# First phase of a transformer-and-experts kernel: block 0 of the token tiles is queued freely, the router's weight parts lie side by side, transposes get one more slot, TensorE gets filler matmuls at its start

## The chip, the cores and the metric

The kernel runs on one core of a Trainium2 chip. Its time is the device time of one execution in microseconds (us). A core has five engines that run side by side, each through its own instructions in their order: TensorE (PE, matmuls; the rows PEld are its weight loads), VectorE (DVE), ScalarE (ACT), GpSimd (POOL) and SyncE (SP, which here only issues DMA transfers). They wait for one another by semaphores.

## The reference

The input is 4096 tokens of width 256. Three residual steps follow each other: a mixture of experts, attention, and the same mixture again.

```python
x = x + 0.5 * ffn(layernorm(x), router_w, rg, ru, rd, sg, su, sd)
x = x + attn(layernorm(x), w_qkv, ln_w, w_proj)
x = x + 0.5 * ffn(layernorm(x), router_w, rg, ru, rd, sg, su, sd)

def ffn(x, ...):                                  # 8 experts, 2 per token, capacity 640
    xn = x * rsqrt(mean(x * x) + eps)
    probs = softmax(xn @ router_w.T)
    top 2 of probs, their weights normalised to a sum of 1
    per expert e, its first 640 tokens in order:
        eout = (silu(xg @ rg[e]) * (xg @ ru[e])) @ rd[e], times the token's weight
    routed = those rows added to their tokens
    shared = (silu(x @ sg) * (x @ su)) @ sd       # sg, su: 256 x 2048, sd: 2048 x 256
    return shared + routed
```

Attention works in groups of 64 tokens with 16 heads of width 16, a causal mask, and normalised queries and keys.

## The kernel before

All matmuls run in float16 on numbers that are split in two: a high half `hi`, rounded to float16, and a low half `lo`, the rounded rest. `split` makes both from a float32 tile (ScalarE the high half, L105; VectorE the low half, L106). A product is the sum of three of the four products of halves, `TERMS`: hi by hi, hi by lo, lo by hi.

The kernel has four phases. Phase a takes the tokens in 32 tiles of 128, which form 8 blocks of 4 tiles. Each tile is loaded (L669), normalised, transposed into the block's buffer `xb` (hi of two column halves, then lo of both), and routed. In the same phase the shared feed-forward runs for the blocks 0 to 3. Phase b is the 8 experts, phase c attention of the 32 tiles together with shared blocks 4 to 7 and the second router, phase d the experts again and the last shared block.

The shared feed-forward (`shared`) goes through 16 steps `c` for a block. A step has gate and up matmuls (`pgu`, L337, twelve of 512 columns), then `sl` by ScalarE (silu, L348) and VectorE (L350), `hh` and `hl` (the split of `sl`, L352 and L353), and the twelve down matmuls of the step before it (`po`, L361).

A tile of phase a goes through `tile1` and `front_steps`. `stats` computes mean and variance on VectorE (`st` L145, `mv` L146, `ve` L148) and the reciprocal root on POOL (`rstd` L150); `normed` makes `z` (L162). The four tiles of block 0 (`PEB = 1`) are then transposed by TensorE: `turn` makes two transposes into `ptx` (L186), a ScalarE copy of the high half (L187) and a VectorE subtraction for the low half (L188). Every later tile is written by `two` as halves into `X` (L169, L170) and transposed by a DMA that SP issues (`flip`, L179); two yields later `logits` multiplies it with the router's weights `rwt` (`pl`, L637, six matmuls of 8 columns per tile) and ScalarE copies the result into `L` (L224). After four tiles `route` picks the two experts of each token (L240, L241 and on), computes weights on POOL and the places in the experts' buffers, and POOL scatters the rows (L318).

The order of the work has two sources. The program yields between steps, and `Tiles.steps` and `drive` let several tiles advance by one step each between the steps of the shared feed-forward. Then the build's planner (`schedule_with_timeline_sim=True`) sets the order of each engine's instructions by its own estimates. It is bound by the data, and by `issue_after`: what is built inside `behind(True, 0, 1)` may not stand ahead of the two instructions in `self.latest`. `turn` sets `latest` to its ScalarE copy and its VectorE subtraction; later the feed-forward sets it (L348, L350). In `Tiles.steps` every step of every tile is put behind `latest` as soon as there is one, that is from the second tile's statistics on.

PSUM has three buffers for gate and up matmuls, two for `po` in this phase, and three shared by `ptx`, `pl`, the router's small matmuls and the transposed router weights `prt`. `rwt` is a tile of [128, 2, 2, 8]: before the change the first index of the two is the part (hi, lo), the second the half of the 256 columns.

The shared weights are loaded and split in eight portions by `load_shared`, the first at once from ScalarE's DMA queue, the others from SP's queue, which also carries the token tiles.

Of the kernel before, what the change touches and what calls it, by code (L numbers as in the profile page):

```python
# [8 lines left out]
F32 = mybir.dt.float32  # L9
# [6 lines left out]
ALU = mybir.AluOpType  # L16
# [4 lines left out]
P = 128  # L21
# [8 lines left out]
E = 8  # L30
# [4 lines left out]
TERMS = ((0, 0), (0, 1), (1, 0))  # L35


class Net:
# [70 lines left out]
    def load_router(self, router_w):  # L109
        nc = self.nc  # L110
        r = self.raw.tile([E, H], F32, name="rtr", bufs=1)
        nc.sync.dma_start(out=r, in_=router_w)
        self.rwt = self.cst.tile([P, 2, 2, E], F16, name="rwt")
        p = self.m1([P, 2, E], F32, "prt")
        for k in range(2):
            nc.tensor.transpose(p[:, k, :], r[:, k * P:(k + 1) * P], self.ident[:E, :E])
        self.split(self.rwt[:, 0], self.rwt[:, 1], p)

    def load_shared(self, sg, su, sd):

# [54 lines left out]
    def flip(self, xp, xt=None):  # L175
# [3 lines left out]
        self.nc.sync.dma_start_transpose(out=xt, in_=xp[:, 0:2 * H])  # L179
        return xt  # L180

    def turn(self, z, xt):

        p = self.m1([P, 2, P], F32, "ptx")
        for k in range(2):
            self.nc.tensor.transpose(p[:, k, :], z[:, k * P:(k + 1) * P], self.ident)  # L186
        i = self.nc.scalar.copy(xt[:, 0:2], p)  # L187
        j = self.nc.vector.tensor_tensor(out=xt[:, 2:4], in0=p, in1=xt[:, 0:2], op=ALU.subtract)  # L188
        self.latest = [i.ins, j.ins]

    @contextmanager
    def behind(self, on=True, *engines):
# [24 lines left out]
    def logits(self, fb, t, xt):  # L217

        nc = self.nc
        p = self.m1([P, E], F32, "pl")  # L220
        self.project(p, lambda a, k: xt[:, 2 * a + k, :], self.rwt, TERMS)
        if t == 0:
            fb["L"] = self.sm.tile([P, 4, E], F32, name="L")
        nc.scalar.copy(fb["L"][:, t, :], p)  # L224

    def route(self, R, b, fb):

        nc = self.nc
        sm = self.sm
        mv, rstd = fb["mv"], fb["rstd"]  # L230
        rs = sm.tile([P, 4], F32, name="rs")
        nc.gpsimd.tensor_tensor(out=rs, in0=rstd, in1=rstd, op=ALU.mult)
        nc.gpsimd.tensor_tensor(out=rs, in0=rs, in1=mv[:, :, 1], op=ALU.mult)
        nc.gpsimd.tensor_scalar_add(rs, rs, RMS_EPS * UP ** 2)
        nc.gpsimd.tensor_tensor(out=rs, in0=rs, in1=self.mhalf[:, :4], op=ALU.pow)
        L = fb["L"]
        mx = sm.tile([P, 4, E], F32, name="mx")
        ix = sm.tile([P, 4, E], U32, name="ix")
        for t in range(4):
            nc.vector.max(out=mx[:, t, :], in_=L[:, t, :])  # L240
            nc.vector.max_index(out=ix[:, t, :], in_max=mx[:, t, :], in_values=L[:, t, :])  # L241
        dl = sm.tile([P, 4], F32, name="dl")
        nc.vector.tensor_tensor(out=dl, in0=mx[:, :, 1], in1=mx[:, :, 0], op=ALU.subtract)
        nc.gpsimd.tensor_tensor(out=dl, in0=dl, in1=rs, op=ALU.mult)
        nc.gpsimd.tensor_scalar_mul(dl, dl, 1.0 / WS)
        nc.gpsimd.tensor_tensor(out=dl, in0=self.e1, in1=dl, op=ALU.pow)
        w1 = sm.tile([P, 4], F32, name="w1")
        nc.gpsimd.tensor_scalar_add(w1, dl, 1.0)
        nc.gpsimd.tensor_tensor(out=w1, in0=w1, in1=self.mone, op=ALU.pow)
        nc.gpsimd.tensor_scalar_mul(w1, w1, 0.5 / WS)  # L250
        nc.gpsimd.tensor_tensor(out=dl, in0=dl, in1=w1, op=ALU.mult)
        nc.gpsimd.tensor_tensor(out=w1, in0=w1, in1=dl, op=ALU.subtract)
        ef = sm.tile([P, 4, 2], F32, name="ef")
        nc.vector.tensor_copy(ef, ix[:, :, 0:2])
        yield
        oh = sm.tile([P, 4, 2, E], F32, name="oh")
        nc.vector.tensor_tensor(
            out=oh, in0=ef.unsqueeze(3).to_broadcast([P, 4, 2, E]),
            in1=self.iota8.unsqueeze(1).unsqueeze(1).to_broadcast([P, 4, 2, E]), op=ALU.is_equal)
        M = sm.tile([P, 4, E], BF16, name="M")  # L260
        nc.vector.tensor_tensor(out=M, in0=oh[:, :, 0, :], in1=oh[:, :, 1, :], op=ALU.add)
        yield
        pp = self.m1([P, 4, E], F32, "pp")
        nc.tensor.matmul(pp, lhsT=self.tri, rhs=M, start=True, stop=False)
        for t in range(1, 4):
            nc.tensor.matmul(pp[:, t:4], lhsT=self.ones, rhs=M[:, 0:4 - t], start=False, stop=False)
        nc.tensor.matmul(
            pp, lhsT=self.ones, rhs=R["run"].unsqueeze(1).to_broadcast([P, 4, E]), start=False, stop=True)
        n4 = sm.tile([P, E], F32, name="n4")
        nc.vector.tensor_reduce(out=n4, in_=M.rearrange("p t e -> p e t"), axis=AX.X, op=ALU.add)  # L270
        nc.vector.tensor_tensor(out=R["run"], in0=R["run"], in1=n4, op=ALU.add)
        pk = sm.tile([P, 4, 2, E], F32, name="pk")
        nc.vector.tensor_tensor(
            out=pk, in0=oh, in1=pp.unsqueeze(2).to_broadcast([P, 4, 2, E]), op=ALU.mult)
        pos = sm.tile([P, 4, 2], F32, name="pos")
        nc.vector.tensor_reduce(out=pos, in_=pk, axis=AX.X, op=ALU.add)
        yield
        df = sm.tile([P, 4, 2], F32, name="df")
        nc.vector.scalar_tensor_tensor(
            out=df, in0=ef, scalar=float(CAP), in1=pos, op0=ALU.mult, op1=ALU.add)  # L280
        nc.vector.tensor_scalar(
            out=pos, in0=pos, scalar1=float(CAP), scalar2=8192.0, op0=ALU.is_ge, op1=ALU.mult)
        nc.vector.tensor_tensor(out=df, in0=df, in1=pos, op=ALU.add)
        di = sm.tile([P, 4, 2], I32, name="di")
        nc.vector.tensor_copy(di, df)
        yield
        if b == NB - 1:
            self.limits(R)
            yield
        for t in range(4):  # L290
            with self.tc.issue_after(self.anchor.ins) if self.anchor else nullcontext():
                self.scatter(R, b, fb, t, di, w1, dl, ef)
            yield
# [346 lines left out]
    def front_steps(self, y, t, new_fb, keep=None):  # L640
        fb = new_fb(t)
        self.stats(y, fb["mv"][:, t, :], fb["rstd"][:, t:t + 1])
        yield
        X = self.xs.tile([P, XW], F32, name="X")
        xp = X[:, 0:H].bitcast(F16)
        fb["X"][t] = X
        z = self.normed(y, fb["mv"][:, t, :], fb["rstd"][:, t:t + 1], keep is not None)
        xt = fb["xb"][:, :, t * P:(t + 1) * P]
        if fb["pe"]:
            self.turn(z, xt)  # L650
            fb["n"] += 1
            for _ in range((3 - t) * GAP_A + 1):
                yield
        with self.behind(fb["pe"], 0, 1):
            self.two(xp, z, keep is not None)
        if keep is not None:
            self.nc.sync.dma_start(out=keep, in_=y)
        yield
        if not fb["pe"]:
            self.flip(xp, xt)  # L660
            yield
            yield
        self.logits(fb, t, xt)
        fb["n"] += not fb["pe"]
        yield
# [7 lines left out]
class Tiles:  # L673
# [12 lines left out]
    def steps(self):  # L686

        if self.slot == self.nxt * self.gap and self.nxt < self.count:
            self.live.append(self.make(self.nxt))
            self.nxt += 1  # L690
        for g in list(self.live):
            with self.held.behind(self.held.latest is not None, 0, 1) if self.held else nullcontext():
                r = next(g, "end")
            if r == "end":
                self.live.remove(g)
            elif r == "stall":
                return
            yield
        self.slot += 1
# [10 lines left out]
def run_slots(tiles, until):  # L710
    while not until():
        for _ in tiles.steps():
            pass
# [22 lines left out]
def macaron(ctx, tc, x, w_qkv, ln_w, w_proj, router_w, rg, ru, rd, sg, su, sd, out):  # L736
    nc = tc.nc
    x = x.rearrange("b s h -> (b s) h")
    out = out.rearrange("b s h -> (b s) h")
    n = Net(ctx, tc)  # L740
# [47 lines left out]
    with n.phase("a", BT, 2, 16):  # L788
        n.ident = n.at.tile([P, P], F32, name="ident")
        make_identity(nc, n.ident)  # L790
        weights = n.load_shared(sg, su, sd)
        next(weights)
        n.load_router(router_w)
        tiles = Tiles(tile1, 32, GAP_A, n)
        run_slots(tiles, ready(1, 0))
        next(weights)
        for b in range(NA):
            run_slots(tiles, ready(1, b))
            main = all_shared((1, b), b, x, R1["acc"])
            drive(fed(main, weights) if b == 0 else main, tiles, RATE_A)  # L800
        run_slots(tiles, tiles.done)
# [26 lines left out]
PEB = 1  # L828
# [29 lines left out]
```

## Time and profile before

| what | value |
|---|---|
| median of 3 runs | 1824.61 us (1823.98 to 1827.08) |
| profiled execution, its own time | 1828.36 us |
| profiled execution, span from first to last instruction | 1826.6 us |
| busy: TensorE, VectorE, ScalarE, POOL | 97%, 66%, 52%, 41% |
| first gate matmul of the shared feed-forward | 17.57 us |
| first gate matmul of an expert in phase b | 284.2 us |
| DMA engines, mean busy share up to 17.57 us | 0.81 |

The profile is of one execution. Its times count from the start of the span. A row of the timeline has the start (us), the time until the last of its instructions ends (us), engine, source line, operation, what is written and read, how many instructions of the kind are in the row, and in brackets how long the engine idled before and what ended that. `L337` is line 337 of the kernel before. Matmuls overlap in the records, so that the time from one start to the next is the better measure of one. A row of the view by windows has the stretch (us), its length, the busy time and count of TensorE, its weight loads, VectorE, ScalarE and POOL, the share of TensorE's full clock that was granted, the DMA engines' busy share, and GB/s.

### The profile page before, as it was taken

Reading aid. Unit: us, or ns where it says so; the run is one execution under the profiler, and the core shown is the slowest. Engines: PE = TensorE matmul, PEld = TensorE weight load, DVE = VectorE, ACT = ScalarE, POOL = GpSimd, SP = SyncE. Lnnn points to the kernel's source line nnn. Section 1 sums busy time; section 2 is a strip of 40 time slices with the busy share of each in tenths; the row PEclk is TensorE's granted clock in tenths of the full one; section 3 lists DMA queues with packets and bytes.
Section 4 is the critical chain, followed back from the end, with each engine's and each line's share of the span. In section 5 each row is a group of like instructions: output and inputs, shape, how many; then the busy total and the mean of one; then the engine's idle time right before and its main releaser. Section 6 shows DMA issues by size and latency. Waiting matters only on the chain.

```text
span 1826.6 us, 37514 instructions
## 1 busy us (share of the span) xinstructions
PE 1778.0 (97%) x13724; PEld 1197.1 (66%) x13724; DVE 1198.9 (66%) x2891; ACT 951.6 (52%) x2055; POOL 754.5 (41%) x1072
## 2 busy tenths in 40 slices
PE   6999999999999899999999999999999999999998
PEld 3555657777777556666666666666655677777765
DVE  6665545666666567787777877887756566666643
ACT  4433334555555466666666666666333455555542
POOL 4666630122111334566767676776430011113210
PEclk9999999999999999999999999999999999999999
DMA  6244132455443356767576776756213144455420
GB/s 196 80 114 114 32 88 63 108 125 120 115 108 87 83 82 99 134 111 148 118 144 118 133 146 117 144 100 130 51 28 73 32 111 108 111 122 122 102 44 12
DMA packets 439193, 185.95 MB, mean 102 GB/s; under 512 B 302305, under 2 KB 436125, under 8 KB 439008
## 3 DMA queue, kind: packets, MB, share of 16 engines
q1 hardware_dynamic: 420528, 161.60, 40.8%
q0 software_dynamic: 17664, 21.17, 6.5%
q8 instruction: 107, 1.75, 0.4%
q10 hardware_dynamic: 816, 0.79, 0.1%
q14 instruction: 78, 0.64, 0.1%
HBM read 78.95 MB, written 42.21 MB: 66 GB/s over the span
## 4 chain that ended last, share of the span: by engine, by line
PE 47%; issue 21%; POOL 12%; DVE 10%; DMA 5%; ACT 3%; SPq 1%; another core or an unknown queue 1%; POOLq 0%; DVEq 0%; ACTq 0%
PE pgu L337 29%; PE po L361 15%; POOL xg L318 3%; DVE sl L350 2%; DMA acc<-eo,eidscatter 2%; DVE sl L345 1%; DVE hl L353 1%; POOL X L316 1%; POOL rstd L150 1%; POOL acc L460 1%; PE pqk L637 1%; POOL S L584 1%; POOL xa L170 1%; ACT sl L344 1%
## 5 line engine op out<-in xcount | busy, mean ns | idle before, releaser
L337 PE MATMUL pgu<-xb,sgu 128*128 128x512 f16 x3072 | 742.2, 380 | 15.5 <-DVE sl L345 8.6
L352 ACT CAST hh<-sl 128x512 f16<-128x512 f32 (+2 forms) x512 | 273.1, 534 | 481.5 <-DVE sl L350 465.5
L337 PE MATMUL pgu<-xe,wc 128*128 128x384 f16 (+1 forms) x3072 | 497.0, 299 | 0.0
L337 PEld LDWEIGHTS <-sgu 128*128 128x128 f16 x3072 | 293.4, 98 | 291.7 <-issue 24.2
L350 DVE SCALAR_TENSOR_TENSOR sl<-pgu,sl 128x512 f32<-128x512 f32 (+2 forms) x512 | 300.7, 588 | 244.8 <-PE pgu L337 213.3
L353 DVE TENSOR_TENSOR hl<-sl,hh 128x512 f16<-128x512 f32 (+2 forms) x512 | 310.8, 607 | 152.6 <-ACT hh L352 147.2
L361 PEld LDWEIGHTS <-hh 128*128 128x128 f16 x3328 | 320.8, 98 | 107.9 <-ACT hh L352 7.3
L337 PEld LDWEIGHTS <-wc 128*128 128x128 f16 x3072 | 300.6, 98 | 92.0
L361 PE MATMUL po<-sdw,hh 128*128 128x256 f16 x2048 | 350.0, 273 | 3.4 <-ACT hh L352 2.2
L361 PE MATMUL po<-sdw,hl 128*128 128x256 f16 x1024 | 247.6, 273 | 6.6 <-DVE hl L353 5.9
L361 PE MATMUL po<-wd,hh 128*128 128x256 f16 x1280 | 223.6, 273 | 0.0
L460 POOL DMA_INDIRECT out_dram<-eo,eidscatter x40 | 65.2, 1629 | 341.5 <-DVE eo L459 331.8
L348 ACT ACTIVATE sl<-pgu 128x384 f32<-128x384 f32 (+1 forms) x336 | 158.9, 473 | 73.0 <-PE pgu L337 43.8
L361 PEld LDWEIGHTS <-hl 128*128 128x128 f16 x1664 | 162.8, 98 | 48.5 <-DVE hl L353 14.7
L460 POOL DMA_INDIRECT acc<-eo,eidscatter x40 | 66.2, 1655 | 293.4 <-DVE eo L459 283.7
L318 POOL DMA_INDIRECT xg<-X,di x128 | 131.3, 1026 | 54.8 <-issue 27.8
L361 PE MATMUL po<-wd,hl 128*128 128x256 f16 x640 | 152.5, 273 | 0.6 <-DVE hl L353 0.6
L345 DVE SCALAR_TENSOR_TENSOR sl<-sl,pgu 128x512 f32<-128x512 f32 x176 | 120.0, 682 | 48.1 <-ACT sl L344 46.9
L344 ACT ACTIVATE sl<-pgu 128x512 f32<-128x512 f32 x176 | 104.2, 593 | 44.9 <-PE pgu L337 35.4
L105 ACT ACTIVATE wc<-re 128x512 f16<-128x512 f32 x128 | 80.5, 629 | 68.9 <-PE pgu L337 59.4
L106 DVE SCALAR_TENSOR_TENSOR wc<-re,wc 128x512 f16<-128x512 f32 x128 | 88.3, 690 | 22.0 <-ACT wc L105 21.8
L584 POOL TENSOR_TENSOR S<-S,amx 128x1024 f32<-128x1024 f32 x32 | 62.1, 1939 | 79.0 <-DVE amx L583 72.0
(150 smaller groups left out, 1713.6 us busy)
## 6 DMA issues: line engine op xcount, KB each, us to landing
re<-in_L_ffn_rg_dram SPq DMA_DIRECT2D x128, 128.0 KB
re<-in_L_ffn_ru_dram SPq DMA_DIRECT2D x128, 128.0 KB
re<-in_L_ffn_rd_dram SPq DMA_DIRECT2D x128, 128.0 KB
y<-acc SPq DMA_DIRECT2D x64, 128.0 KB
y<-in_L_attn_x_dram SPq DMA_DIRECT2D x32, 128.0 KB
acc<-xr SPq DMA_DIRECT2D x16, 256.0 KB
out_dram<-xr SPq DMA_DIRECT2D x16, 256.0 KB
x<-y SPq DMA_DIRECT2D x28, 128.0 KB
```

What stands on the lines that cost most here:

```text
L105: nc.scalar.mul(hi, src, WS)
L106: nc.vector.scalar_tensor_tensor(out=lo, in0=src, scalar=WS, in1=hi, op0=ALU.mult, op1=ALU.subtract)
L318: i = nc.gpsimd.indirect_dma_start(out=R["xg"][:, :], out_offset=bass.IndirectOffsetOnAxis(ap=di[:, t, k:k + 1], axis=0), in_=X, in_offset ...
L337: nc.tensor.matmul(p, lhsT=wc[:, w, i, k, :], rhs=x[:, 2 * a + k, :], start=(j == 0), stop=(j == 5))
L344: nc.scalar.activation(s, p, AF.Tanh, scale=0.5 / XP)
L345: nc.vector.scalar_tensor_tensor(out=s, in0=s, scalar=1.0, in1=p, op0=ALU.add, op1=ALU.mult)
L348: self.latest[0] = nc.scalar.activation(s, p, AF.Silu, scale=1.0 / XP).ins
L350: self.latest[1] = nc.vector.scalar_tensor_tensor(out=s, in0=ps[1], scalar=1.0 / XP / (2.0 * XP if tanh else 1.0), in1=s, op0=ALU.mult, op ...
L352: nc.scalar.copy(h[0], s)
L353: nc.vector.tensor_tensor(out=h[1], in0=s, in1=h[0], op=ALU.subtract)
L361: nc.tensor.matmul(o, lhsT=h[a][:, t * P:(t + 1) * P], rhs=wd[:, w], start=(c == 0 and j == 0 and t % 2 == 0), stop=(c == nch - 1 and j == 2),
L460: i = nc.gpsimd.indirect_dma_start(out=R["acc"][:, :], out_offset=bass.IndirectOffsetOnAxis(ap=ids[:, t:t + 1], axis=0), in_=eo, in_offset ...
```

## The change

- `Tiles.steps` keeps each tile's number and puts its steps behind `latest` for tiles of block 1 and later; the tiles of block 0 are not held.
- `rwt` is laid out with the column half first, so that its high and low parts are neighbours. `logits` multiplies the high half of a tile with both parts at once (16 columns), and the low half with the high part (8 columns): four matmuls per tile. The two partial sums stay apart in `L`; `route` adds them with one VectorE instruction per block.
- A tile of phase a that is transposed by DMA waits three yields, not two, before its logits. Tiles of phase c keep two.
- `keep_going(n)` issues n matmuls of the constant tile `ones` (128 columns, bfloat16) into a buffer that nothing reads: 20 before the router's weights are transposed, 16 after, and 5 after each `turn`, 56 in all.

```diff
@@ load_router
-        self.split(self.rwt[:, 0], self.rwt[:, 1], p)
+        self.split(self.rwt[:, :, 0], self.rwt[:, :, 1], p)
@@ Net
+    def keep_going(self, n):
+        p = self.m1([P, P], F32, "idle")
+        for _ in range(n):
+            self.nc.tensor.matmul(p, lhsT=self.ones, rhs=self.ones, start=True, stop=True)
@@ turn
         self.latest = [i.ins, j.ins]
+        self.keep_going(5)
@@ logits
-        p = self.m1([P, E], F32, "pl")
-        self.project(p, lambda a, k: xt[:, 2 * a + k, :], self.rwt, TERMS)
+        p = self.m1([P, 2, E], F32, "pl")
+        for k in range(2):
+            nc.tensor.matmul(
+                p, lhsT=xt[:, k, :], rhs=self.rwt[:, k], start=(k == 0), stop=False, skip_group_check=True)
+            nc.tensor.matmul(
+                p[:, 0], lhsT=xt[:, 2 + k, :], rhs=self.rwt[:, k, 0], start=False, stop=(k == 1),
+                skip_group_check=True)
         if t == 0:
-            fb["L"] = self.sm.tile([P, 4, E], F32, name="L")
-        nc.scalar.copy(fb["L"][:, t, :], p)
+            fb["L"] = self.sm.tile([P, 4, 2, E], F32, name="L")
+        nc.scalar.copy(fb["L"][:, t], p)
@@ route
-        L = fb["L"]
+        L = sm.tile([P, 4, E], F32, name="Ls")
+        nc.vector.tensor_tensor(out=L, in0=fb["L"][:, :, 0], in1=fb["L"][:, :, 1], op=ALU.add)
@@ front_steps
             self.flip(xp, xt)
-            yield
-            yield
+            for _ in range(2 if keep is not None else 3):
+                yield
@@ Tiles.steps
-            self.live.append(self.make(self.nxt))
+            self.live.append((self.nxt, self.make(self.nxt)))
             self.nxt += 1
-        for g in list(self.live):
-            with self.held.behind(self.held.latest is not None, 0, 1) if self.held else nullcontext():
-                r = next(g, "end")
+        for one in list(self.live):
+            with self.held.behind(one[0] >= 4 * PEB, 0, 1) if self.held else nullcontext():
+                r = next(one[1], "end")
             if r == "end":
-                self.live.remove(g)
+                self.live.remove(one)
@@ macaron, phase a
         next(weights)
+        n.keep_going(20)
         n.load_router(router_w)
+        n.keep_going(16)
         tiles = Tiles(tile1, 32, GAP_A, n)
```

## The prediction

> **What bounds the kernel now.** I read the page first: TensorE is busy 97% of the span, and in the row of slices only the first slice (45.7 us each) is clearly below 9.
>
> ```profile
> span 1826.6 us, 37514 instructions
> PE 1778.0 (97%) x13724; PEld 1197.1 (66%) x13724; DVE 1198.9 (66%) x2891; ACT 951.6 (52%) x2055; POOL 754.5 (41%) x1072
> PE   6999999999999899999999999999999999999998
> ```
>
> So time is won only where TensorE waits, runs at a low clock, or has work taken off it. The diff touches the first phase (to 284.2 us, where the first expert's gate matmul starts) and, through `logits` and `route`, the attention phase. The waits of TensorE in two windows, 0 to 17.6 us and 17.6 to 284.2 us (us in total, times, longest), come next:
>
> ```profile
> PE ptx L186 <- DVE z L162: 11.4, 4, 3.0
> ...
> PE pgu L337 <- DVE sl L350: 4.2, 5, 1.5
> PE pl L637 <- DMA xb<-X: 3.3, 4, 2.1
> ```
>
> The 11.4 us are the four tiles of block 0, taken one behind the other. The timeline shows one turn of that chain, and where the real work begins:
>
> ```profile
> 4.01 0.43 DVE L145 BATCH_NORM_STATS2 st<-y 128x6 f32<-128x256 f32 x1 [1.75 <-DMA y<-in_L_attn_x_dram]
> 4.47 0.18 DVE L146 BATCH_NORM_AGGREGATE mv<-st 128x2 f32<-128x6 f32 x1
> 4.69 0.15 DVE L148 TENSOR_SCALAR ve<-mv 128x1 f32<-128x1 f32 x1
> 4.93 0.58 POOL L150 TENSOR_TENSOR rstd<-ve,mhalf 128x1 f32<-128x1 f32 x1 [2.19 <-DVE ve L148]
> 5.54 0.41 DVE L162 TENSOR_SCALAR z<-y,mv,rstd 128x256 f32<-128x256 f32 x1 [0.70 <-POOL rstd L150]
> 6.01 0.69 PE L186 MATMUL ptx<-ident,z 128*128 128x128 f32 x2 [2.99 <-DVE z L162]
> 6.74 0.37 ACT L187 CAST xb<-ptx 128x256 f16<-128x256 f32 x1
> 7.14 0.42 DVE L188 TENSOR_TENSOR xb<-ptx,xb 128x256 f16<-128x256 f32 x1 [1.19 <-ACT xb L187]
> 7.48 0.42 DVE L145 BATCH_NORM_STATS2 st<-y 128x6 f32<-128x256 f32 x1
> ...
> 17.57 2.72 PE L337 MATMUL pgu<-xb,sgu 128*128 128x512 f16 x6 [0.16 <-ACT xb L187]
> 20.09 0.34 PE L637 MATMUL pl<-rwt,xb 128*128 128x8 f16 x6
> ```
>
> The statistics of tile 1 start at 7.48, only after the last step of tile 0 (7.14), although VectorE idles in between: a turn costs 3.47 us, four of them put the first gate matmul at 17.57. These six matmuls then take 2.52 us (17.57 to 20.09), 0.42 each, while the same six later take 1.46 with their tail, 0.216 from start to start. The clock is seen once more, in the windows view, behind the longest wait for a transpose:
>
> ```profile
> 147.83 0.32 PE L637 MATMUL pl<-rwt,xb 128*128 128x8 f16 x6 [2.07 <-DMA xb<-X]
> ```
> ```profile
> 147.78:151.20 3.42, 3.37 (x19) 1.99 (x20) 1.64 (x13) 1.08 (x3) 0.00 (x0) 0.50 0.42 115
> ```
>
> TensorE idled 2.07 us, and for the next 3.42 us the granted clock was 0.50: the wait costs 2.07 + 1.7.
>
> **The change part by part.**
>
> *Block 0 not in line.* In the order of the changed program VectorE does: statistics of tile 0, then st1, z0, aggregates of 1, st2, st3, subtract 0, z1, aggregates, z2, subtract 1, z3, subtracts 2 and 3, and then the low half of the first weights. With the durations above (0.43, 0.18, 0.15, z 0.41, subtract 0.42), the row's gaps, and 0.7 us from ve to z over POOL: z0 ends at 5.95, subtract 0 (its ScalarE copy ends at 7.11) at 7.9, z1 at 8.3, z2 at 9.8, subtract 1 at 10.2, z3 at 10.7. From the end of z to the high half in `xb` tile 0 took 5.95 to 7.11, so z3 gives 11.85 and the first gate matmul 11.9. Bounds: if no step waits, VectorE has 5.7 us of work up to z3, giving 10.9; if the z of tiles 1 to 3 each wait 0.7 us for POOL as now, 14. **-5.7 (-3.6 to -6.7).** What it leans on: the loads of tiles 1 to 3 must have landed. They are issued 0.55 us apart from 1.27, tile 0 landed at 3.98, and the 16 DMA engines are 81% busy up to 17.57, so tile 3 by about 6 is needed at 6.8. Weights follow in SP's same order; the x loads behind them, now held by z (5.98, 9.42, 12.85 at present), only start earlier.
>
> The route of block 0 now stands ahead of the first `sl` on VectorE: add, 4 maxima, 4 indices, some 1.7 us of small rows (four maxima 0.36 in a row). `sl` waits for the second gate group anyway; I get 0.6 us late there, and three PSUM buffers of gate matmuls cover it. **+0.3 (0 to +1).**
>
> *TensorE filled.* 36 fillers of 128 columns stand ahead of the first transpose; at the slow clock 0.42 x 128/512 = 0.107 each, 3.9 us with the router's two transposes 0.25: from 1.2 (the memset of `ones` ends at 1.15) to 5.3, before z0 at 5.95. If each took twice that (weight load not hidden; but the logits pairs repeat every 0.027 us at the slow clock), the first transpose and all behind it would be 3.3 us late. The five after each transpose, 0.5 us, lie beside the ScalarE copy; the last five end at 11.9, level with it.
>
> What they earn is the slow start: 17.57 to 21.5 at half rate, nine gate matmuls x 0.21 = 1.9. [...] **-1.0 (0 to -1.9).**
>
> *Router parts side by side.* Six `pl` matmuls become four per tile. Six take 0.155 us from start to start of what follows (83.03 to 83.18), so two fewer save 0.053; 64 tiles, 3.4 us. Half lies in the first phase, wholly on TensorE's path; in the attention phase TensorE is busy 769 of 788 us. **-3.0 (-1.7 to -3.4).** Added are 16 adds on VectorE (128x32; like the smallest rows 0.15, at most L243's mean 0.6) and copies of 16 columns for 8 on ScalarE (now 0.16): beside TensorE, on engines at 66% and 52%. Their cover is the route being several steps ahead of its scatters; without it 16 x 0.15 = 2.4. 0.
>
> *One more slot behind the transposes.* In the built orders, the matmuls between a transpose's issue and its logits are worth (0.216 per gate, 0.109 per down matmul) 1.2 to 5.6, mostly 2.6 us before, and 5.9 to 7.6 for most tiles after; but the first tile of each block stays at 0.9 to 3.9. The chain of waits has these transposes landing 2.3 to 3.6 us after their issue. So the 3.3 us of waiting and the 1.7 of half clock mostly go. **-4.2 (0 to -5.0).** What moves later: scatters, and the first expert's `tag` load, by 12 gate matmuls, one step of 3.9 us of TensorE. The scatters now end at 253, the transposed expert input is issued by 259.3, its matmul starts at 284.2: the cover is about 20 us. VectorE's wait there for expert weights (TensorE loses 1.4 us behind it at 264 and 268) is in the same place of the order. **+0.5 (0 to +3).**
>
> *Sum:* -5.7 + 0.3 - 1.0 - 3.0 - 4.2 + 0.5 = **-13.1**. The expert phase (TensorE 325 of 328 us) and the last pass it on. The profiled execution took 1828.36 (span 1826.6), 3.75 above the median of the runs, 1824.61; on the median that is **1811.5**. Nothing is taken for the 4.2 us of waits for `sl`: the order differs in each, either sign.
>
> **The rivals.**
>
> *Start only* (chance 0.20): the transposes' waits come back at the first tiles of the blocks, whose cover is no larger than before, and the clock stays slow: -5.7 + 0.8 - 1.7 = -6.6, 1818.0. For it: that 0.9 to 3.9 us. Against: the longest wait now had only 1.2 us of cover.
>
> *Given back at the seam* (0.10): TensorE reaches the experts early and stands for what SP and POOL bring; SP waited 23 us (231 to 254) behind the scatters there. About 1823. Against it the 20 us of cover, shifted by 4.
>
> *Slower* (0.07): the first transposed tile of each of the seven later blocks idles TensorE 2.07 us and drops its clock, 3.8 us each, 26.6 in all; against -8.9 of the other parts that is +17.7, 1842. It decides from four such stalls on: 8.9 + 3.65 is 3.3 of them. For it: the thin cover. Against: the present order, with thin cover at most tiles, shows one.
>
> **How the numbers follow.** Likeliest 0.63, 1811.5, own range 1806 to 1816. 0.2% of 1824.6 is 3.65 us, about what a measurement of this kernel can tell from no change. Start only is nearly all on the faster side; the seam is same; so faster 0.82, same 0.11, slower 0.07. The range takes the ends of the costs below (-19: 1805.5) and start only with a late tile 3 above: 1805.5 to 1821.
>
> **What would show it.** First gate matmul near 11.9; no ptx wait of 3 us; the first six gate matmuls at 0.22 (clock right) or 0.42 each; no `pl` wait on `xb` of over 1 us and no stretch of clock 0.50 inside the span; 256 `pl` matmuls; first expert matmul near 272. Wrong if that start is above 15, if new waits of `pgu` on `sl` exceed 4.2 us by several, or if the expert matmul starts as late as 280.

## The result

The changed kernel takes 1819.28 us (median of eight executions, 1818.27 to 1820.05) against 1825.65 us for the kernel before beside it (1823.98 to 1827.08): a ratio of 0.9965, 95% interval 0.9956 to 0.9975. It is faster by 6.4 us; forecast were 13.1. The start gave what was forecast. The other parts did not.

The page of the changed kernel: the span, TensorE's row, and its row of 40 slices.

```profile
span 1817.6 us, 37398 instructions
PE 1778.5 (98%) x13652; PEld 1199.6 (66%) x13652; DVE 1190.9 (66%) x2907; ACT 949.4 (52%) x2055; POOL 753.4 (41%) x1072
PE   8999999999999899999999999999999999999998
```

The first slice has gone from 6 to 8. TensorE has 72 instructions fewer (128 fewer `pl`, 56 fillers more); its busy time is no smaller, since the fillers' 7.2 us count as busy.

What TensorE waited for up to its first gate matmul (12.20 us), and from there to the first expert matmul at 274.22 us (waits in us in total, times, longest):

```profile
PE ptx L191 <- DVE mv L146: 1.2, 1, 1.2
...
PE ptx L191 <- DVE ve L148: 0.9, 1, 0.9
```
```profile
PE po L373 <- DVE ve L148: 2.3, 1, 2.3
PE pgu L349 <- ACT sl L360: 2.0, 1, 2.0
PE po L373 <- DVE hl L365: 1.6, 1, 1.6
PE pgu L349 <- DVE sl L362: 0.8, 1, 0.8
...
PE pl L228 <- DMA xb<-X: 0.3, 1, 0.3
```

The four waits for `z` of 11.4 us are down to two of 2.1 together, and the wait of `pl` on `xb` from 3.3 to 0.3. But in place of the latter there are longer waits of `po` and `pgu`: 7.1 us with a row of 0.4 left out here, where those rows summed to 4.8 before.

The timeline of the changed kernel's start, a few of its rows:

```profile
6.31 0.41 DVE L162 TENSOR_SCALAR z<-y,mv,rstd 128x256 f32<-128x256 f32 x1
6.87 0.66 PE L191 MATMUL ptx<-ident,z 128*128 128x128 f32 x2 [1.23 <-DVE mv L146]
...
10.41 0.40 DVE L162 TENSOR_SCALAR z<-y,mv,rstd 128x256 f32<-128x256 f32 x1
12.20 1.37 PE L349 MATMUL pgu<-xb,sgu 128*128 128x512 f16 x3
```

The last `z` ends at 10.81 (10.7 in the forecast), and the first gate matmul starts at 12.20 (11.9).

For the rest the span is cut at four events in TensorE's records: the first gate matmul, the first expert matmul of phase b, the last one of phase b, and the first expert matmul of phase d. A run of the kernel before, profiled again beside other experiments (e12 below; its own time 1827.02, 0.57 above the median of its 12 executions), is a better partner than the profile of before, whose own time lies 2.7 us above the median. The forecast for the body is the sum of the route, the fillers, half the router part (the other half is put down to the attention phase), the slot and the seam: 0.3 - 1.0 - 1.5 - 4.2 + 0.5.

| us | before | before, again | changed | forecast of the difference |
|---|---|---|---|---|
| first gate matmul at | 17.57 | 17.95 | 12.20 | -5.7 |
| body of the first phase | 266.61 | 264.74 | 262.03 | -5.9 |
| phase b | 314.76 | 314.72 | 314.04 | 0 |
| attention phase | 843.49 | 843.29 | 845.37 | -1.5 |
| phase d | 314.08 | 314.46 | 314.14 | 0 |

Against the second profile the start is 5.75 us earlier, the body of the first phase 2.7 shorter instead of 5.9, and the attention phase 2.1 longer instead of 1.5 shorter. So there are two losses to explain, 3.2 and 3.6 us.

### The profile page after: what moved, and what is told of

Its sections match the earlier page's. It is cut to its first block, busy times and chain, and to the rows that moved or that the text cites. A ratio compares the mean times of both kernels' runs of the same rounds, so it can differ in the third digit from the quotient of the medians.

```text
span 1817.6 us, 37398 instructions
## 1 busy us (share of the span) xinstructions
PE 1778.5 (98%) x13652; PEld 1199.6 (66%) x13652; DVE 1190.9 (66%) x2907; ACT 949.4 (52%) x2055; POOL 753.4 (41%) x1072
## 5 line engine op out<-in xcount | busy, mean ns | idle before, releaser
L373 PE MATMUL po<-sdw,hl 128*128 128x256 f16 x1024 | 249.8, 273 | 14.0 <-DVE hl L365 11.4
```

Source lines behind the costliest of these rows:

```text
L373: nc.tensor.matmul(o, lhsT=h[a][:, t * P:(t + 1) * P], rhs=wd[:, w], start=(c == 0 and j == 0 and t % 2 == 0), stop=(c == nch - 1 and j == 2),
```

## The experiments

Kernels of a group ran on one chip beside the kernel before. That kernel took 1834.81 us beside the first group (e1 to e4), 1827.17 beside the second (e5 to e8), 1826.16 beside the third (e9 to e12), 1830.91 beside the fourth (e13 to e16) and 1827.19 beside the last (e17, e18); so ratios compare within a group, and across groups with care. "Gate" is the start of the first gate matmul, "body" the stretch from there to the first expert matmul, "attention" the stretch between the two expert phases; these three are from one profile each.

| run | gate | body | attention | time, us | ratio to before (95%) |
|---|---|---|---|---|---|
| e1 router part alone | 18.23 | 274.55 | 850.08 | 1841.47 | 1.0036 (1.0023 to 1.0050) |
| e2 router part in the first phase only | 11.79 | 265.03 | 844.86 | 1819.78 | 0.9921 (0.9907 to 0.9934) |
| e3 changed, without the slot | 11.86 | 266.53 | 847.96 | 1828.29 | 0.9966 (0.9954 to 0.9978) |
| e4 e2 with scatters held | 12.04 | 255.58 | 843.58 | 1811.70 | 0.9879 (0.9864 to 0.9894) |
| e5 changed | 12.18 | 263.15 | 845.30 | 1820.96 | 0.9965 (0.9953 to 0.9977) |
| e6 changed, maximum held behind hl | 12.42 | 263.52 | 841.60 | 1816.74 | 0.9941 (0.9928 to 0.9955) |
| e7 e6 with scatters held | 11.88 | 255.53 | 840.49 | 1809.58 | 0.9907 (0.9892 to 0.9922) |
| e8 changed, without fillers | 10.79 | 262.42 | 847.59 | 1821.72 | 0.9969 (0.9957 to 0.9981) |
| e9 changed, without the router part | 12.24 | 260.82 | 841.40 | 1815.90 | 0.9948 (0.9931 to 0.9964) |
| e10 changed, block 0 in line | 17.98 | 267.60 | 846.79 | 1831.05 | 1.0027 (1.0014 to 1.0040) |
| e11 e4 without the slot | 12.19 | 256.68 | 842.44 | 1811.40 | 0.9921 (0.9904 to 0.9938) |
| e12 before | 17.95 | 264.74 | 843.29 | 1826.45 | 1.0004 (0.9995 to 1.0013) |
| e13 before with scatters held | 18.54 | 258.82 | 844.10 | 1822.54 | 0.9948 (0.9931 to 0.9964) |
| e14 e10 with scatters held | 17.94 | 255.86 | 847.45 | 1822.12 | 0.9952 (0.9936 to 0.9969) |
| e15 e9 with scatters held | 11.57 | 255.21 | 842.84 | 1811.43 | 0.9894 (0.9877 to 0.9910) |
| e16 router part alone | 17.91 | 271.85 | 849.35 | 1839.89 | 1.0052 (1.0035 to 1.0068) |
| e17 changed | 12.29 | 262.25 | 844.60 | 1819.74 | 0.9963 (0.9951 to 0.9975) |
| e18 changed, without the slot | 12.14 | 263.80 | 845.51 | 1819.69 | 0.9958 (0.9945 to 0.9972) |

### Where the waits of the first phase come from

Behind the longest wait of TensorE in the changed kernel stands a queue that the forecast never looked at. Its timeline around 137 us, rows of POOL, VectorE and TensorE:

```profile
135.05 0.98 POOL L330 DMA_INDIRECT xg<-X,di  x1 [0.30 <-issue]
136.33 0.98 POOL L330 DMA_INDIRECT xg<-X,di  x1 [0.30 <-issue]
...
137.45 0.59 POOL L150 TENSOR_TENSOR rstd<-ve,mhalf 128x1 f32<-128x1 f32 x1
...
138.07 0.41 DVE L162 TENSOR_SCALAR z<-y,mv,rstd 128x256 f32<-128x256 f32 x1 [5.08 <-POOL rstd L150]
138.49 0.66 DVE L365 TENSOR_TENSOR hl<-sl,hh 128x512 f16<-128x512 f32 x1
...
139.21 0.10 PEld L373 LDWEIGHTS <-hl 128*128 128x128 f16 x1 [2.76 <-DVE hl L365]
139.21 0.28 PE L373 MATMUL po<-sdw,hl 128*128 128x256 f16 x1 [2.27 <-DVE ve L148]
```

POOL issues the eight scatters of a block one behind the other, 0.98 us each and 1.28 apart, some ten us in all (127.2 to 137.3 here). The next tile's `rstd` stands behind them in POOL's queue; `z`, next in VectorE's order, idles 5.08 us for it; `hl` of the feed-forward stands behind `z`; and TensorE stands 2.27 us for `hl`, whose end (139.15) is what its weight load waits for; the row of the matmul names `ve`, which ends on VectorE just then. The wait list names the last releaser and hides the rest of the chain. Eight scatters in a row are called a train from here on. In the kernel before it is the same train, near the same place:

```profile
140.63 0.97 POOL L318 DMA_INDIRECT xg<-X,di  x1 [0.30 <-issue]
141.60 1.13 POOL L150 TENSOR_TENSOR rstd<-ve,mhalf 128x1 f32<-128x1 f32 x2
142.25 0.93 DVE L162 TENSOR_SCALAR z<-y,mv,rstd 128x256 f32<-128x256 f32 x2
144.14 3.84 SPq L179 DMA_TRANSPOSE xb<-X  x2
```

There the late `z` made the transposes late, and `pl` at 147.83 was the first to find out. The slot gives `pl` more time, so `hl` finds out instead.

To take the cause away, the scatters are put behind the latest `rstd` (the step that builds them is already held behind `self.anchor`, L291 before, which is unset in the first phase):

```diff
@@ stats
-        nc.gpsimd.tensor_tensor(out=rstd, in0=ve, in1=self.mhalf[:, :1], op=ALU.pow)
+        i = nc.gpsimd.tensor_tensor(out=rstd, in0=ve, in1=self.mhalf[:, :1], op=ALU.pow)
+        if self.name == "a":
+            self.anchor = i
```

The first group tells this apart from the transposes' cover. e1 is the kernel before with the router lines of the change alone. e2 is the changed kernel with six matmuls per tile, as before, in the attention phase. e3 is the changed kernel with two yields for three. e4 is e2 with the edit above.

> The kernel before with the router's parts side by side alone (four logits matmuls for six, the add in route), nothing else of the change. Theory A (this edit makes the planner put the maximum over the attention scores, amx, 1.2 us, ahead of hl on VectorE, in seven tiles of the attention phase): the stretch from the last expert matmul of the first experts to the first of the second experts is about 845.5 us, where before had 843.5, against a gain of 1.7 in the first phase: the time is that of before within 1.5 us. Rival (the longer attention phase comes from the shifted start, not from this edit): that stretch is 842 to 843.5 and the time 3 us below before.

> The whole change, but in the attention phase the logits stay six matmuls and no add (the parts are side by side in the first phase alone). Theory A: the attention stretch is 843.5 again, first phase as in the changed kernel; the time is 2 us below the changed kernel, some 8.4 below before. Rival: the stretch stays 845.4 and the time is within 0.5 us of the changed kernel or above it.

> The changed kernel with two yields behind a transpose, as before, in place of three. My prediction's step: 4.2 us are lost again, and the logits wait for their transposes by 3 us in all. Theory B (those waits were the tail of a VectorE stall: z waits for rstd, which stands on POOL behind a train of eight scatters of 10 us): the slot is worth under 1.5 us, TensorE still has its longest stall of 2 to 2.5 us near 137 us, and a stretch of clock 0.50 behind it.

> As the kernel with the parts side by side in the first phase alone, and each scatter of the first phase is held behind the latest rstd on POOL, so that the train of eight is cut into two, four and two. Theory B: VectorE's stall of 5 us at the third train goes, TensorE's stalls of 1.8, 2.4 and 2.1 us in the first phase fall by at least half, no clock of 0.50 inside the span, and the time is 3 to 6 us below the kernel with uncut trains. Rival (the half clock comes a fixed 126.3 us after the array got full clock, whatever TensorE does): it is there again, at the same distance. Rival (the scatters come later and the experts wait): the first expert matmul is later than 274 us.

e4 has a body of 255.58 us where e2 has 265.03, and is 8.1 us faster (1811.70, 1819.78). e1 missed its expectation in size: the router part alone makes the kernel 6.7 us slower. e2 decided little: its attention phase of 844.86 us lies between the two expectations, and its time, 15.0 below before, has no changed kernel beside it. Of e3's two expectations each came in half. Its waits of `pl` on `xb` were there (4.6 us), as my prediction's step had it, but the ratio is that of the changed kernel (0.9966, 0.9965), so no 4.2 us were lost. The long stall near 137 us and the half clock behind it, which theory B had, were absent: the longest wait of the phase is 1.89 us, at 262.8, and the profile's mean granted clock is 1.000.

The cut does the same to every kernel that got it. e13 is the kernel before with it, e14 the changed kernel with block 0 in line and the cut, e15 the change without its router part and with the cut; e16 is e1 on another chip.

> The kernel before with one thing added: in the first phase the scatters may not stand ahead of the latest reciprocal root on POOL. My theory, that these trains cause most of the waits of TensorE in the first phase, gives 256.5 to 258.5 us from the first gate matmul to the first expert matmul (264.7 and 266.6 in the two profiles of before; 1.9 of it is the slow start), no wait of over 1.2 us between 25 and 240 us, and 1818 to 1820 for the whole, ratio 0.9955 to 0.997. The rival, that the thin cover of the transposes is what makes them wait, keeps pl waits of 1 to 2 us on xb: 261 or more, ratio 0.998 or more.

> The changed kernel with block 0 in line again, and with the scatters held behind the latest reciprocal root. If the 5.6 us that the in-line start cost in the body of the first phase were trains, they go: 255.5 to 257.5 us from the first gate matmul (near 17.9) to the first expert matmul, and the whole 5.5 to 7.5 us slower than the same with the free start, 1818 to 1820. If they are a cost of the start itself, the stretch stays above 260 us and the whole above 1822.

> The change without its router part, with the scatters held behind the latest reciprocal root. The two gains should add, one being in the first phase and one in the attention phase: first gate matmul at 12.2, 256 to 258 us to the first expert matmul (six router matmuls per tile cost 1.7 more there), 841 to 843.5 in the attention phase, the whole 1810 to 1812.5, 3.5 to 6 us below the change without its router part. If the router part's loss came from the trains too, nothing is left between this and the kernel with both the router part and the cut: 1811 to 1812.

> The router part alone once more, on another chip, where the kernel before takes about 1826. If the long first phase (274.55 us) belongs to the program's order: 273 to 275.5 again, with a wait of over 3 us near 57 us, and 1836 to 1842, ratio 1.005 or more. If it belonged to that chip: 265 to 269, 1826 to 1831, ratio 1.000 to 1.003.

e13, POOL's rows in its timeline: the first and the last of four scatters, and an `rstd` that need not wait for the other four (137.73 to 142.67).

```profile
129.87 1.11 POOL L321 DMA_INDIRECT xg<-X,di  x1 [0.17 <-POOL rs L235]
...
133.85 0.97 POOL L321 DMA_INDIRECT xg<-X,di  x1 [0.30 <-issue]
134.99 0.58 POOL L151 TENSOR_TENSOR rstd<-ve,mhalf 128x1 f32<-128x1 f32 x1
```

The waits of TensorE in e13 from 18 to 274 us, all but one of 0.2:

```profile
PE pgu L340 <- DVE sl L353: 2.2, 3, 1.1
PE pp L267 <- DVE M L264: 0.6, 1, 0.6
PE po L364 <- DVE hl L356: 0.4, 1, 0.4
PE pgu L340 <- ACT sl L351: 0.3, 1, 0.3
...
```

No wait of `pl` on `xb` is left, with two slots as before. So those waits were not for want of cover: they were the trains. e13 is 8.4 us faster than the kernel before; its body is 0.3 above the expected stretch and its time 2.5, on a chip that runs the kernel before at 1830.91; the ratio, 0.9948, is just below what was expected. Bodies with the cut: 255.21 to 258.82 us in six kernels. Without it: 260.82 to 274.55. e15's is 0.8 below the expected stretch, its time inside. The changed kernel with the cut and nothing else was not run.

The router part alone has its long body on both chips (274.55, and 271.85, 1.2 below what was expected), so it belongs to the program. Its worst train stands as follows in e1's timeline, and at the same place in e10 (57.41 for the last scatter, 59.04 for `z`):

```profile
57.49 0.97 POOL L329 DMA_INDIRECT xg<-X,di  x1 [0.30 <-issue]
58.46 1.13 POOL L150 TENSOR_TENSOR rstd<-ve,mhalf 128x1 f32<-128x1 f32 x2
59.11 0.41 DVE L162 TENSOR_SCALAR z<-y,mv,rstd 128x256 f32<-128x256 f32 x1 [5.60 <-POOL rstd L150]
...
61.38 0.93 PE L348 MATMUL pgu<-xb,sgu 128*128 128x512 f16 x3 [3.55 <-DVE sl L361]
```

### The attention phase

The router part makes TensorE's work smaller, but the planner answers with another order on VectorE. In five of the 32 tiles of the attention phase, by VectorE's rows in the traces (the expectations speak of seven), the maximum over the scores (`amx`) came after `hl` before the change and comes ahead of it after. All ten profiles of kernels with the router part in that phase and nothing holding `amx` have the new order, in the same five tiles; no other profile has it. The changed kernel's timeline in one such tile:

```profile
849.77 0.68 DVE L590 TENSOR_TENSOR S<-psc,mask 128x512 f32<-128x512 f32 x1
...
850.48 1.22 DVE L595 TENSOR_REDUCE amx<-S 128x16 f32<-128x1024 f32 x1
...
851.62 0.68 DVE L365 TENSOR_TENSOR hl<-sl,hh 128x512 f16<-128x512 f32 x1
...
852.36 0.28 PE L373 MATMUL po<-sdw,hl 128*128 128x256 f16 x1 [0.74 <-DVE hl L365]
```

`hh` is ready at 850.5 (its cast starts at 849.89 and takes 0.62), `hl` starts 1.1 us later, behind `amx`, and TensorE idles 0.74 for it. The same tile in e9, the change without its router part:

```profile
847.03 1.28 DVE L584 TENSOR_TENSOR S<-psc,mask 128x512 f32<-128x512 f32 x2
...
848.23 0.68 DVE L359 TENSOR_TENSOR hl<-sl,hh 128x512 f16<-128x512 f32 x1
...
848.83 1.21 DVE L589 TENSOR_REDUCE amx<-S 128x16 f32<-128x1024 f32 x1
```

The second group undoes the order alone. e5 is the changed kernel once more. e6 is the changed kernel with `amx` built behind the next to last `hl`; e7 has the cut of the trains besides; e8 leaves the fillers out.

```diff
@@ gate_up
-        nc.vector.tensor_tensor(out=h[1], in0=s, in1=h[0], op=ALU.subtract)
+        self.hl = getattr(self, "hl", [])[-1:] + [nc.vector.tensor_tensor(out=h[1], in0=s, in1=h[0], op=ALU.subtract).ins]
@@ the maximum over the scores
-        nc.vector.tensor_reduce(out=mx, in_=S, axis=AX.X, op=ALU.max)
+        with self.tc.issue_after(self.hl[0]):
+            nc.vector.tensor_reduce(out=mx, in_=S, axis=AX.X, op=ALU.max)
```

> The changed kernel itself, as the reference for the runs beside it: 6.4 us below before, or on another chip that difference within 3 us.

> The changed kernel with amx held behind the hl that it had passed (issue_after), so that in the seven tiles VectorE does hl first, as in the kernel before; four logits matmuls everywhere. Theory A: TensorE's waits of 0.9 us, one per block, in the attention phase are gone, that stretch is 2.5 to 5 us shorter than in the changed kernel beside it, and the time falls by as much. Rival (the longer attention phase is the added instruction in route, or chance): under 1 us.

> The same with the trains of scatters cut as well: the two gains add up: 10 to 16 us below the changed kernel, the attention stretch as short as with amx held, the first phase's 255 to 257 us from the first gate matmul to the experts' first.

> The changed kernel without the 56 filler matmuls. If the fillers earn what the trace shows (three gate matmuls at half rate in place of nine): 1.3 us slower than the changed kernel, the first six gate matmuls 0.42 us apart again, the first of them at 11.9 to 12.2. If they delay the transposes: as fast or faster, the first gate matmul at 11.5 or before.

e6 is 4.2 us faster than e5, 3.7 of it in the attention phase (841.60, 845.30). VectorE has the order of before again in the five tiles; in two others the hold moves `amx` one `hl` later than before. The costliest groups on the page show the waits for `hl` in one row; first the changed kernel, then e6 (busy us, mean ns, idle before, and what ended most of it):

```profile
L373 PE MATMUL po<-sdw,hl 128*128 128x256 f16 x1024 | 249.8, 273 | 14.0 <-DVE hl L365 11.4
```
```profile
L373 PE MATMUL po<-sdw,hl 128*128 128x256 f16 x1024 | 250.3, 273 | 10.5 <-DVE hl L365 7.9
```

e7, with both edits, takes 1809.58 us (1807.62 to 1812.05) where the kernel before took 1827.17 and the changed one 1820.96: the shortest time of all kernels here (e4 and e15 have lower ratios, beside longer times of the kernel before), and faster than both kernels of this case.

### The parts one by one

The third group takes parts out of the changed kernel: e9 the router part, e10 the free start (the condition in `Tiles.steps` is again the one of before); e11 is e4 with two yields; e12 is the kernel before.

> The change without its router part: six matmuls of 8 columns per tile and no adds, as before; block 0 not in line, fillers and the additional slot stay. My theory: the router part costs time in the attention phase because it moves the maximum over the scores ahead of hl on VectorE. Without it the stretch from the last expert matmul to the next expert stage is 843 to 844.5 us (845.3 with it), no turn of that phase has po waiting for hl longer than before, and the whole is 0.5 to 2.5 us faster than the changed kernel: 1817 to 1819.5, ratio to the kernel before about 0.9955. The rival, that the router part saves its 0.05 us per tile as predicted and the attention phase differs by chance: 846.5 or more in that stretch, and 1 to 3 us slower than the changed kernel, ratio 0.997 to 0.998.

> The changed kernel with the tiles of block 0 put in line again; all else of the change stays. If the free start is what most of the gain is: the first gate matmul at 17 to 18.5 us, and the whole about 5 us slower than the changed kernel: 1824.5, ratio to the kernel before 0.999 to 1.000. If the start only lets TensorE reach sooner what it then waits for: the first gate matmul late by 5 us, but the first expert matmul late by less than 3, ratio 0.997 to 0.998.

> The kernel with the side-by-side router parts in the first phase only and the scatters held behind the latest reciprocal root, but with two slots behind a transpose as before, not three. If the waits that the slot was to take away come from the scatters standing ahead of the roots on POOL, the slot is worth nothing once they are held: the stretch from the first gate matmul to the first expert matmul 255.5 to 257.5 us (255.6 with the slot), no stretch of half clock in it, ratio to the kernel before 0.988 to 0.989. If the slot has a cover of its own to give: pl waits on xb of 1 us and more in four or more tiles, the stretch 259 to 262, ratio 0.990 to 0.992.

> The kernel before as it is, for a second profile beside the others. If the profile of before was of a long execution: the stretches of the first phase and of the experts come shorter by 1 to 3 us together, most in the first phase, with the same stall of TensorE behind the late root near 137 us, and a first gate matmul at 17.5 to 18. If it was not: the same stretches within 0.7 us.

Without the router part the change is better: 0.9948 for 0.9965 with it (measured on another chip), some 3 us, and the attention phase is back at 841.40, even below the expected 843; the whole is 1 us below the expected span too. e10 missed: with block 0 in line the rest of the change is 4.6 us slower than the kernel before on the same chip, and the body is 5.6 longer than the changed kernel's. e14 settles that one: with the trains cut the in-line start costs nothing in the body (255.86), only its 5.8 at the first gate matmul; e14's whole missed the expected 1818 to 1820 and is 0.12 above the bound that I had set, for its attention phase (847.45, the router part's order).

e11 has no half clock behind the start (its mean granted clock is 1.000) and a body of 256.68, 1.1 more than e4, as expected if the trains are the cause; the times agree, 1811.40 and 1811.70. The ratio does not, but the one expected came from the first group's longer kernel before.

The last pair measures the slot on one chip: e17 is the changed kernel, e18 the same with two yields.

> The changed kernel, for the comparison with the run without the slot on the same chip: 1819 to 1821, ratio to before about 0.9965, 262 to 263.2 us from the first gate matmul to the first expert matmul, 845 to 845.6 in the attention phase.

> The changed kernel with two slots behind a transpose, as before. If the slot is worth what was forecast: 4.2 us more than the changed kernel beside it, with pl waits on xb of over 3 us in sum. If, as I now think, the stalls only change their place and the trains remain: 0 to 2 us more in the first phase, pl waits of 1 to 2.5 us in sum, and less waiting of the other matmuls; the attention phase, which the slot does not touch in the program, moves by up to 2.5 us either way with the order that the planner builds.

1819.74 and 1819.69 us. The first waits in the list of e17 from 12 to 275 us, and of e18:

```profile
PE pgu L349 <- ACT sl L360: 2.3, 1, 2.3
PE po L373 <- DVE ve L148: 2.2, 1, 2.2
PE po L373 <- ACT hh L364: 1.5, 1, 1.5
PE pl L228 <- DMA xb<-X: 1.4, 3, 0.5
```
```profile
PE pl L228 <- DMA xb<-X: 5.0, 6, 1.7
PE pgu L349 <- DVE sl L362: 2.5, 1, 2.5
PE pgu L349 <- ACT sl L360: 0.6, 1, 0.6
```

The slot does to its own row what it was said to do, 5.0 us to 1.4, and the other rows of the list grow from 3.1 us to 7.9 (with rows of 1.0 and 0.9 not shown). e17's body is 1.5 us shorter all the same: e18's has a stretch of half clock, from 259.98, which e17's has not, and e18's profile is of the longest of its five executions (1821.66). I had expected `pl` waits of 1 to 2.5 us in e18; they are twice that.

## Why the prediction was wrong by half

- *Block 0 not in line, -5.7: right.* 12.20, 12.18 and 12.29 us for the first gate matmul in three profiles, against 17.57 and 17.95. The loads were there; VectorE's interleaved order ran as worked out, 0.3 us later. What the sum lacked is that a start five us earlier also shifts where the trains fall: undone inside the changed kernel (e10) it is worth about 11 us (1.0027 for 0.9965), while with the trains cut (e14) the body is as short as with the free start.
- *Fillers, -1.0: nothing that shows.* The times without and with are 1821.72 (e8) and 1820.96 (e5). e8's first gate matmul starts at 10.79, 1.4 earlier, and its clock is full only at 14.55, so that the gate matmuls up to there run at half rate (three take 1.44 us, against 0.81 in the changed kernel once its clock is full); e5's is full at 14.44. Against the changed kernel's profile some 0.5 us of the 1.4 are tile 0's load, which landed later there (its statistics start at 4.78, in e8 at 4.28). Some 0.8 are VectorE's order: without fillers it does `z` of tile 1 (7.20) ahead of tile 0's subtraction (7.64), with them the subtraction comes first (8.07) and `z` behind it (8.42). Little more than 0.1 is left for fillers that stand in the way of a transpose. No run shows the -1.0: the clock is full from 13.36 in the changed kernel's profile, from 12.12 in e17's (where it was full once before, from 5.29) and from 14.44 in e5's, against 14.55 without fillers. The last section has the stretches ahead of it.
- *Router parts side by side, -3.0: wrong in sign for the attention phase.* The step that failed is "0" for what the edit adds. It costed the added instructions, and compared positions in TensorE's order only; what moved was VectorE's. Ten profiles with the router part's order have 844.60 to 850.08 us in the attention phase (mean 847.0); eight without it 841.40 to 844.86 (843.25); the two that held `amx` in its place 841.60 and 840.49. So in the changed kernel the order costs 3.7 us (e6 against e5). With it undone the matmuls saved show: e6 is 1.7 us shorter there than e12, with waits of TensorE of the same sum in phases b and c (20.7 and 20.9 us; the changed kernel has 23.6, with 3.3 us more for `hl`). The kernels with the longest attention phases (e1 and e16, 849 to 850 us) lose more than that; where, was not followed. What tips the planner was not tried. One candidate is in the traces: the add needs the logits of a whole block, so that VectorE does the four maxima and indices in a row behind it (857.10 to 859.14 in the changed kernel), where before it did those of each tile as they came (868.00 and 888.59). The "0" did not look at that.
- *One more slot, -4.2: nothing, with the cause misread.* "The 3.3 us of waiting and the 1.7 of half clock mostly go" took the wait's last releaser, the transpose, for its cause. The wait went and came back on `po` and `pgu`. The half clock came back too, in the changed kernel's view by windows (length, TensorE, its weight loads, VectorE, ScalarE, POOL, clock share, the DMA engines' busy share, GB/s):

```profile
139.65:143.07 3.42, 3.42 (x13) 1.51 (x11) 2.98 (x19) 1.52 (x3) 0.85 (x5) 0.50 0.51 136
```

  And before's 1.7 us was no steady cost in the first place. In e12, the same program, `pl` waits at the same point and the clock stays full. First the 3.41 us ahead of before's half clock, then the stretch of e12 with its wait:

```profile
144.37:147.78 3.41, 1.39 (x10) 0.71 (x8) 2.02 (x6) 1.11 (x2) 2.24 (x4) 1.00 0.41 74
```
```profile
145.18:148.59 3.41, 1.61 (x17) 1.18 (x18) 1.04 (x2) 0.45 (x2) 1.04 (x2) 1.00 0.39 75
146.97 0.30 PE L637 MATMUL pl<-rwt,xb 128*128 128x8 f16 x6 [1.92 <-DMA xb<-X]
```

- *Seam, +0.5: about right.* TensorE's waits there are 1.97 us up to 256.3 and 0.77 up to 262.5, for 0.28, 1.10 and 0.33 in before (+1.0) and 1.27 and 1.18 in e12 (+0.3).
- *Rivals.* "Start only", 1818.0, comes nearest, and in its own way: what the slot takes away does come back, and the clock with it, though on other matmuls than the first tiles' transposes. Neither the seam nor seven stalls of 3.8 us appeared.
- *Sum.* The low ends of the prediction's parts add up to -17.0, not to the -19 that its range names; nothing hangs on it. Against e12's profile the start gave -5.75, the body -2.7 for -5.9, the attention phase +2.1 for -1.5, phases b and d -1.0 for 0: -7.4. The medians say -6.4.

## What to carry to other kernels

Follow a wait past the engine that ended it, up to the first queue in which something unrelated stands ahead: here eight DMA issues on POOL ahead of a 0.6 us `rstd`. While such a train is there, shaving covers and slots only moves the stall to the next reader, and every shift of the schedule deals the trains anew; holding the train in pieces gave 7.2 to 8.4 us (e7 against e6, e4 against e2, e13 against before), more than the whole change. Where a planner orders the work, an edit must be compared in the built order on every engine, in every phase that shares the function, since here two small matmuls fewer on TensorE moved a 1.2 us VectorE instruction ahead of what TensorE waits for.

## What the runs showed of the hardware

- In the profiles of before and of the changed kernel an indirect scatter takes 0.98 us of POOL's rows in the median and up to 2.24, with 0.30 to the next in most places; the eight of a block take 10.1 to 12.1 us in the first phase, and what stands behind them in POOL's queue waits (`rstd` at 137.45 above, behind the last scatter, which starts at 136.33).
- The length of a wait alone did not tell whether the half clock followed. Behind before's wait of 2.07 us (up to 147.83) and the changed kernel's of 2.27 (up to 139.21) stands a stretch of 3.42 us at 0.50. In e12, the program of before, the wait at the same point is 1.92 us, and the clock is 1.00 from 141 to 151. In e17, the program of the changed kernel, the longest wait is 2.3 us; its mean clock of 0.999 has room for one such stretch, and that one is in the start, from 8.71. Ahead of the half clock TensorE was busy for 1.39 of 3.41 us in before and for 1.15 in the changed kernel (136.24 to 139.65); in e12's stretch with its wait it was busy for 1.61. Whether that decides was not shown. The time since the clock rose does not: before and the changed kernel both had 126.29 us of full clock up to there (from 21.49 and from 13.36), but e4, with a mean clock of 1.000, has no such stretch.
- In the start of the changed kernel, being busy for over half of 3.41 us did not bring TensorE the full clock (2.52 us from 3.12, 2.18 from 6.54), nor did 4.09 us without a break from 1.20 (the 36 fillers and the router's transposes), behind which e17 had it. Its first three gate matmuls, from 12.20, still take 1.37 us where the next three take 0.81. The full clock came at 13.36, behind 3.41 us in which TensorE was busy throughout.
- In e17 the fillers' clock is not kept through the transposes. The view by windows of its start, in the same columns:

```profile
5.29:8.71 3.42, 0.94 (x11) 0.61 (x8) 2.37 (x9) 1.93 (x4) 1.03 (x2) 1.00 1.09 379
8.71:12.12 3.41, 3.04 (x21) 2.71 (x22) 2.08 (x8) 1.00 (x3) 2.65 (x6) 0.50 0.91 285
12.12:15.50 3.38, 3.38 (x33) 1.82 (x31) 3.19 (x18) 1.29 (x7) 0.42 (x3) 1.00 1.08 374
```

  Full at 5.29 after the 36 fillers, half at 8.71 behind a stretch with only 0.94 us of TensorE's work, full again at 12.12, just ahead of the first gate matmul. In the changed kernel's profile the clock turned full only at 13.36: with the same program, three gate matmuls ran at half rate there (1.37 us) and none in e17 (clock 1.00 from 12.12).
